# Graph network, first layer: attribute loads issued in one burst per group instead of in lots of four

## The chip, the cores and the metric

The kernel runs on one core of one Trainium2 chip. The metric is the device time in microseconds of one execution. The engines are TensorE (PE, with its weight loads shown as PEld), VectorE (DVE), ScalarE (ACT), GpSimd (POOL) and SyncE (SP). DMAs are issued from the queues of SP, ACT and POOL; "SPq" and "ACTq" in the profile are the instructions of these queues that issue them.

## The reference, cut to what matters

Four blocks run one after the other on 6250 nodes with 256 features, each adding its result to x: a message-passing layer over 106250 edges, a mixture of experts routed by a graph attention, a second message-passing layer, and a second mixture of experts. The change lies in the first of them:

```python
def _L0_gnn_ref(x, edge_index, edge_attr, u, batch, W1, b1, W2, b2):
    row, col = (edge_index[0], edge_index[1])
    h = jnp.concatenate([x[row], edge_attr], axis=1)
    h = jax.nn.relu(h @ W1 + b1)
    agg = jax.ops.segment_sum(h, col, num_segments=N_NODES)
    cnt = jax.ops.segment_sum(jnp.ones((h.shape[0],), h.dtype), col, num_segments=N_NODES)
    agg = agg / jnp.maximum(cnt, 1.0)[:, None]
    out = jnp.concatenate([x, agg], axis=1)
    return jax.nn.relu(out @ W2 + b2)

x = x + _L0_gnn_ref(_layernorm(x, axis=-1), edge_index, edge_attr_256, ...)
```

All arrays are float32; edge_attr has 106250 rows of 256. The edges are sorted by their target node (col).

## The kernel before

Before the layer, a short stage makes y = layernorm(x) @ W1[:256] + b1 for all nodes and writes it to DRAM (`y_dram`). Then the layer walks over windows of 128 target nodes. There are 49 windows; since the edges are sorted, each window's edges are one run of rows, and the kernel takes 18 tiles of 128 edges for each, cut into three groups of six tiles. So there are 147 groups (`groups1`), and the loop over q is what the change touches. The windows come in seven blocks of seven.

For a group q, the work on the engines is this:

- `load_sources(q)`: six gathers on POOL (`gather`, L1184) bring the rows of y of the edges' source nodes into one of four buffers (`ring`, tile h). The gathers for group q+2 stand in iteration q; the buffer was last read by `add_up(q - 2)`.
- `load_attr(q)`: the attribute rows (tile ea, three buffers) come by 12, 12 or 8 DMAs, for the three groups of a window in turn. Each covers 32 partitions in rows of 256 bytes. The order of their engines is SP, ACT, SP, ACT in each run of four, and SP alone in a third run; so a group has 8, 8 or 4 on SP and always 4 on ACT. The first row of the window is read from a table (`start_of`, L1094) into a register of both queues.
- `turn(q)` (L1613): DVE transposes the loaded rows in blocks of 32 (et <- ea). It stands one iteration ahead of its use, and frees the buffer of ea.
- `hidden(q, j)`: PE multiplies two tiles with the lower half of W1 (helper `mm`, L1170, ph <- w1b, et); three calls make the group.
- `join(q)`: DVE adds the product to the gathered rows (L1631, h <- ph, h), ACT applies relu (L1632).
- `equal(q)`: DVE compares the edges' targets with the lanes of the window (L1283); `add_up(q)`: PE adds the rows up per node (L1650), two iterations after the group's products.

Beside that, three generators advance by one step at fixed places of an iteration (`steps`):

- `work`: the end of a window (`end_of`): mean (ACT L1663, o), transposes (PE L1164, copied by ACT L1165), product with W2, layer norm for the next block (ACT L1685 ln_rs, DVE L1687 and L1689, ACT L1691 xn, named o in the profile), and the attention's scores (ACT L1702 to L1704). All its small products and transposes share one PSUM buffer.
- `sort`: the sort of the attention's edges by DVE, at the end with transposes and writes of the sorted rows through ACT (L1435 to L1438, low_dram).
- `slow`: `windows()`: counting, then once per block `find_starts` (L1091) and `load_windows`, whose first step reads seven windows' source and target indices on SP: seven reads of `start` (L1094) and fourteen DMAs (L1202, raw_src and raw_dst). These index reads fall into the iterations 8, 23, 37, 51, 65 and 79.

The order of the instructions on every engine is the program's order: `ordered.pin()` at the end of each iteration ties each instruction to the one before it on its engine, DMA issues included. Loads are prepared four groups ahead: iteration q prepares group q+4 once `turn(q + 1)` has freed a buffer, so that what `load_attr` issues waits for that transpose.

In the kernel before, `load_attr` issues nothing itself; it returns the list of its DMAs, and `issue(parts, 4)` takes four from the list at three places of an iteration: after the gathers and before `turn(q + 1)`, in the middle after `hidden(q, 2)`, and at the end after `steps(slow)`. The layer begins with a list of two groups; after eight iterations it is so short that a group's first four leave in the middle of the iteration that prepared it, the next four at its end, and the last four, all of SP, at the first place of the next iteration. ACT's two pairs thus stand on both sides of the work step in the middle of the iteration.

Of the kernel before, what the change touches and what calls it, by code (L numbers as in the profile page):

```python
# [918 lines left out]
def kernel(ctx: ExitStack, tc: tile.TileContext, a: dict, out: bass.AP):  # L919
# [73 lines left out]
    V, SC, TE, GP, SY = nc.vector, nc.scalar, nc.tensor, nc.gpsimd, nc.sync  # L993
# [7 lines left out]
    with ExitStack() as fast:  # L1001
# [23 lines left out]
        def bcast_row(pool, name, ap):  # L1025

            n = ap.shape[0]
            t = pool.tile([P, n], F32, name=name)
            SY.dma_start(t, bass.AP(tensor=ap.tensor, offset=ap.offset, ap=[[0, P], [1, n]]))
            return t  # L1030

        def load_rows(pool, name, ap):

            r, n = ap.shape
            t = pool.tile([P, r // P, n], F32, name=name)
            SY.dma_start(t, ap.rearrange("(c p) n -> p c n", p=P))
            return t
# [13 lines left out]
        if T1 > C1:  # L1051
            V.memset(flat.bitcast(I32)[:, C1:T1], 2**24)
            n = E1 - C1 * P
# [39 lines left out]
        def start_of(w, *also):  # L1093
            return nc.values_load(  # L1094
                start[0:1, w : w + 1], engines=(mybir.EngineType.SP, *also), min_val=0,
                max_val=E1 - WE, skip_runtime_bounds_check_because="it is clamped to that",
            )
# [17 lines left out]
        def load_nodes(engine, t0, t1):  # L1115
            for ps, tt, rows in node_parts(a["x"], t0, t1):
                engine.dma_start(x_all[ps, tt, :], rows)
# [18 lines left out]
        def norm_scale(pool, t0, n):  # L1136

            mv = pool.tile([P, n, 2], F32, name="ln_mv")
            for i in range(n):
                st = pool.tile([P, 6], F32, name="ln_st")  # L1140
                V.bn_stats(st, x_all[:, t0 + i, :])
                V.bn_aggr(mv[:, i, :], st)
            rs = pool.tile([P, n], F32, name="ln_rs")
            V.tensor_scalar(rs, mv[:, :, 1], EPS, None, op0=OP.add)
            SC.activation(rs, rs, AF.Sqrt)
            V.reciprocal(rs, rs)
            return mv, rs
# [12 lines left out]
        def transposed(psum, dst, src, n=2):  # L1160

            pt = psum.tile([P, n, P], F32, name="pt")
            for c in range(n):
                TE.transpose(pt[:, c, :], src[:, c * P : (c + 1) * P], ident)  # L1164
            SC.activation(dst, pt.rearrange("p c k -> p (c k)"), AF.Copy)  # L1165

        def mm(dst, lhs, rhs, n=2):

            for c in range(n):
                TE.matmul(dst, lhs(c), rhs(c), start=c == 0, stop=c == n - 1)  # L1170
# [154 lines left out]
        def load_keys():  # L1325

            for i, raw in enumerate((key, order)):
                edge = a["L0_ffn_edge_index"][i, :].rearrange("(p t) -> p t", t=C2)
                SY.dma_start(raw.bitcast(I32), edge)
# [118 lines left out]
        with ExitStack() as layer:  # L1448
# [45 lines left out]
            def load_attr(q):  # L1494

                w, g = groups1[q]
                parts = []
                ea = wea.tile([P, G1 * 4, 2 * Q], F32, name="ea")
                r = start_of(w, mybir.EngineType.Activation)
                rows = a["edge_attr_256"][bass.ds(r, WE), :]  # L1500
                at = 0
                for i, (first, n) in enumerate(RUNS[g]):
                    part = rows[first * P : (first + n) * P, :]
                    for c in (0, 2, 1, 3):
                        parts.append((
                            SY if c < 2 or i == 2 else SC,
                            ea[c * Q : (c + 1) * Q, at : at + 4 * n, :],
                            part[:, 2 * c * Q : 2 * (c + 1) * Q].rearrange(
                                "(m p) d -> p m d", p=Q
                            ),  # L1510
                        ))
                    at += 4 * n
                return ea, parts

            def issue(parts, n):

                for engine, to, part in parts[:n]:
                    engine.dma_start(to, part)
                del parts[:n]


            with (
                tc.tile_pool(name="w0", bufs=1) as w0,
                tc.tile_pool(name="n0", bufs=3) as wk,
                tc.tile_pool(name="pt0", bufs=3, space=PSUM) as pst,
                tc.tile_pool(name="p0", bufs=3, space=PSUM) as psm,
                tc.tile_pool(name="pq0", bufs=1, space=PSUM) as psq,
            ):
                w1a = load_rows(w0, "w1a", a["L0_gnn_W1"][0:D, :])
                b1 = bcast_row(w0, "b1", a["L0_gnn_b1"])  # L1530
                for b in range(1, NB):
                    load_nodes(SY, b * TB, (b + 1) * TB)
                ahead = {}
                for t0, t1 in parts0:
                    b = t0 // TB
                    mv, rs = norm_scale(wk, t0, t1 - t0)
                    off = wk.tile([P, TB], F32, name="off")
                    V.scalar_tensor_tensor(
                        off[:, 0 : t1 - t0], mv[:, :, 0], -1.0, rs, op0=OP.mult, op1=OP.mult
                    )  # L1540
                    for i in range(t1 - t0):
                        t = t0 + i
                        xn = wk.tile([P, D], F32, name="xn")
                        SC.activation(
                            xn, x_all[:, t, :], AF.Identity, bias=off[:, i : i + 1],
                            scale=rs[:, i : i + 1],
                        )
                        xt = b_all[:, t, :]
                        transposed(pst, xt, xn)
                        pm = psm.tile([P, D], F32, name="pm")  # L1550
                        mm(pm, lambda c: xt[:, c * P : (c + 1) * P], lambda c: w1a[:, c, :])
                        yb = wk.tile([P, D], F32, name="yb")
                        V.tensor_add(yb, pm, b1)
                        SY.dma_start(y_nodes[:, t, :], yb)
                    if t1 == TB:
                        for w in range(TB):
                            count_below(w)
                        find_starts(psq, 0)
                    if b == 1:
                        b2, w1b, w2, *of_gat = load_weights(w0)  # L1560
                        for _ in load_windows(0, psq):
                            pass
                    if b == 2:
                        load_keys()
                    if b == 4:
                        wgx = with_scores(w0, *of_gat)
                    if b >= 4:
                        ahead[b - 4], parts = load_attr(b - 4)
                        issue(parts, len(parts))


            HS = D + 4
            with (
# [24 lines left out]
                NQ1 = len(groups1)  # L1598
# [137 lines left out]
                for q in range(3):  # L1736
                    load_sources(q)
                turn(0)
                LOT = 4
                ordered = Ordered(tc)  # L1740
                for q in range(NQ1 + 2):
                    if 0 < q <= NQ1:
                        join(q - 1)
                    if q < NQ1:
                        hidden(q, 0)
                    steps(keys or sort)
                    if q >= 2:
                        add_up(q - 2)
                        if (q - 2) % NG == NG - 1:
                            work.append(end_of((q - 2) // NG))  # L1750
                    if 3 <= q + 2 < NQ1:
                        load_sources(q + 2)
                    issue(parts, LOT)
                    if q + 1 < NQ1:
                        turn(q + 1)
                    for n in range(q + 2, min(q + 5, NQ1)):
                        if n not in ahead:
                            ahead[n], more = load_attr(n)
                            parts += more
                    if q < NQ1:  # L1760
                        hidden(q, 2)
                    issue(parts, LOT)
                    steps(keys or (sort if q % 4 else []))
                    if q < NQ1:
                        equals[q] = equal(wk, *groups1[q])
                        hidden(q, 4)
                    steps(slow)
                    issue(parts, LOT)
                    ordered.pin()
                while work or sort or slow:  # L1770
                    steps(sort, slow)
# [110 lines left out]
        part = sums.tile([P, 3, T, H], BF16, name="part")  # L1882
        with (
# [17 lines left out]
            for at in range(0, NM * P, D):  # L1901
                n = min(D, NM * P - at)
# [882 lines left out]
        with (  # L2785
# [6 lines left out]
            n = wk.tile([P, NB + 7], F32, name="n")  # L2792
# [61 lines left out]
```

## Time and profile before

| | us |
|---|---|
| median of 10 runs | 3302.36 |
| lowest, highest | 3299.53, 3311.06 |
| the profiled execution, its own time | 3304.03 |
| its span, first to last instruction | 3302.2 |
| first gather of the layer, last relu's end | 102.0, 1260.2 |
| busy in the span: PE, DVE, POOL, ACT | 3004.0, 2185.4, 2277.2, 1184.6 |

The whole profile is of one execution. A line of a group or of a timeline gives the start and length of an instruction, its engine, its line in the kernel, what it writes and reads, and in brackets how long its engine stood idle before it and what ended that. The release is inferred from semaphores; "issue" means that the profile shows nothing that was waited for. DMA-issuing instructions are not counted as busy, and merged lines give the time from the first to the last of them.

### The profile page before, as it was taken

To read this page: it belongs to the slowest core of one execution; us is meant where nothing else is said; L and a number is where in the kernel's file an instruction comes from. 1 tells how busy PE (TensorE), PEld (TensorE's weight loads), DVE (VectorE), ACT (ScalarE), POOL (GpSimd) and SP (SyncE) were. 2 spreads that over 40 slices of the span, in tenths; PEclk is the share of its full clock that TensorE was granted. 3 is DMA by queue.
4 is the path that set the end of the run, shared out by engine and by line. 5 is a ranking of instruction groups with operands and counts; after the bars stand their busy time and mean duration, and the time that the engine had idled before them with its cause. 6 is when DMAs were issued, how large, how long until landed. Compare 5 with 4: busy or idle time off the path is not lost.

```text
span 3302.2 us, 59987 instructions
## 1 busy us (share of the span) xinstructions
PE 3004.0 (91%) x18517; PEld 2361.5 (72%) x18517; DVE 2185.4 (66%) x6516; ACT 1184.6 (36%) x2200; POOL 2277.2 (69%) x2720
## 2 busy tenths in 40 slices
PE   6899999999999989999999999956788888889997
PEld 5677777777777767888888888844566666656675
DVE  6678887888777766887685869962344444444464
ACT  5122222222222223456666668840112112112234
POOL 1577777777777774777776677427777777777772
PEclk8999999999999999999999999965577777777798
DMA  5788998989998873445454535532222222222221
GB/s 176 190 195 196 201 207 191 199 198 205 206 206 204 193 180 101 114 104 137 108 145 107 142 96 154 134 102 53 53 59 59 59 60 55 64 60 59 60 66 30
DMA packets 704935, 423.34 MB, mean 128 GB/s; under 512 B 538699, under 2 KB 647303, under 8 KB 704604
## 3 DMA queue, kind: packets, MB, share of 16 engines
q1 hardware_dynamic: 422972, 201.12, 23.3%
q0 software_dynamic: 88512, 171.58, 22.9%
q10 hardware_dynamic: 193120, 46.69, 7.0%
q8 instruction: 150, 2.46, 0.3%
q14 instruction: 181, 1.48, 0.2%
HBM read 382.75 MB, written 42.50 MB: 129 GB/s over the span
## 4 chain that ended last, share of the span: by engine, by line
PE 57%; POOL 14%; DMA 11%; issue 9%; DVE 5%; ACT 2%; SPq 2%; ACTq 0%; DVEq 0%; POOLq 0%
PE ph L1170 30%; POOL hg L1184 12%; PE py L1170 11%; PE pe L1650 4%; PE pt L1170 4%; DMA hg<-hp_dram,src 3%; PE pe L2714 3%; DMA ea<-in_edge_attr_dram 3%; DMA h<-y_dram,src 1%; PE po L2032 1%; POOL sg L1184 1%; DMA rb<-low_dram 1%; PE pt L1164 1%; PE pa L1955 1%; SPq L1202 1%
## 5 line engine op out<-in xcount | busy, mean ns | idle before, releaser
L1184 POOL DMA_INDIRECT h<-y_dram,src x882 | 860.6, 976 | 368.7 <-issue 212.1
L1184 POOL DMA_INDIRECT hg<-hp_dram,src x831 | 784.8, 944 | 280.5 <-issue 237.4
L1170 PE MATMUL ph<-w1b,et 128*128 128x256 f32 x3528 | 832.0, 388 | 14.7 <-DVE et L1613 9.5
L1184 POOL DMA_INDIRECT sg<-gat_dram,src x612 | 612.0, 1000 | 267.3 <-issue 166.5
L1170 PEld LDWEIGHTS ph<-w1b,et 128*128 128x128 f32 x3528 | 659.7, 192 | 162.3 <-issue 76.1
L2714 PEld LDWEIGHTS pe<-eq,hg 128*128 128x128 f32 x2036 | 397.4, 260 | 295.4 <-issue 142.8
L2714 PE MATMUL pe<-eq,hg 128*128 128x96 f32 (+15 forms) x2036 | 452.7, 354 | 147.9 <-DMA hg<-hp_dram,src 124.2
L2691 DVE TENSOR_SCALAR eq<-px,dst,ew 128x96 f32<-128x96 f32 x831 | 262.6, 369 | 247.1 <-PE pe L2714 145.6
L1170 PE MATMUL py<-w,hh 128*128 128x256 f32 x1568 | 399.5, 393 | 11.7 <-ACT hh L1833 10.3
L1170 PE MATMUL ph<-b_all,w 128*128 128x256 f32 (+1 forms) x1600 | 402.2, 388 | 1.0 <-ACT hh L1833 1.0
L1632 ACT ACTIVATE h<-h 128x1536 f32<-128x1536 f32 x147 | 218.4, 1486 | 503.5 <-DVE h L1631 249.5
L1631 DVE TENSOR_TENSOR h<-ph,h 128x1536 f32<-128x1536 f32 x147 | 258.2, 1756 | 170.4 <-PE ph L1170 123.3
L1170 PEld LDWEIGHTS py<-w,hh 128*128 128x128 f32 x1568 | 282.0, 192 | 49.6 <-ACT hh L1833 15.4
L1170 PEld LDWEIGHTS ph<-b_all,w 128*128 128x128 f32 x1600 | 284.1, 192 | 30.7 <-ACT hh L1833 1.5
L1613 DVE STREAM_TRANSPOSE et<-ea 128x1536 f32<-128x1536 f32 x147 | 260.8, 1774 | 14.6 <-DMA ea<-in_edge_attr_dram 9.7
L1833 ACT ACTIVATE hh<-ph,b 128x256 f32<-128x256 f32 (+1 forms) x400 | 166.9, 466 | 125.6 <-PE ph L1170 106.0
L2010 DVE TENSOR_SCALAR E<-nodes,bits 128x256 bf16<-128x256 bf16 (+5 forms) x612 | 187.8, 348 | 35.6 <-PE po L2032 34.2
L1650 PE MATMUL pe<-h,eq 128*32 128x257 f32 x2496 | 180.8, 394 | 0.0
L1833 ACT ACT_TABLE_LOAD x102 | 130.9, 1283 | 22.8 <-PE ph L1170 12.5
L1165 ACT ACTIVATE b_all<-pt 128x256 f32<-128x256 f32 x147 | 54.0, 377 | 214.9 <-PE pt L1164 211.4
L1170 PE MATMUL py<-ew,g 65*128 65x256 f32 x392 | 128.7, 457 | 1.0 <-DVE miss L2799 1.0
L1650 PEld LDWEIGHTS pe<-h,eq 128*32 128x32 f32 x2496 | 72.6, 111 | 69.5 <-issue 35.2
(358 smaller groups left out, 3941.8 us busy)
## 6 DMA issues: line engine op xcount, KB each, us to landing
ea<-in_edge_attr_dram SPq DMA_DIRECT2D x784, 64.0 KB
ea<-in_edge_attr_dram ACTq DMA_DIRECT2D x392, 64.0 KB
w<-in_L_ffn_W_dram SPq DMA_DIRECT2D x48, 512.0 KB
y<-ys SPq DMA_DIRECT2D x96, 256.0 KB
rb<-low_dram SPq DMA_DIRECT2D x84, 256.0 KB
ea<-in_edge_attr_dram ACTq DMA_DIRECT2D x196, 96.0 KB
ea<-in_edge_attr_dram SPq DMA_DIRECT2D x196, 96.0 KB
h<-y_dram,src POOLq DMA_INDIRECT x882
```

The source lines that it names most:

```text
L1164: TE.transpose(pt[:, c, :], src[:, c * P : (c + 1) * P], ident)
L1165: SC.activation(dst, pt.rearrange("p c k -> p (c k)"), AF.Copy)
L1170: TE.matmul(dst, lhs(c), rhs(c), start=c == 0, stop=c == n - 1)
L1184: GP.indirect_dma_start(out=dst, out_offset=None, in_=table[0:NP, :], in_offset=IndirectOffsetOnAxis(ap=idx, axis=0), **more,)
L1613: V.transpose(et[q].rearrange("p c m k -> p m c k"), ahead.pop(q).rearrange("p m (c k) -> p m c k", c=2),)
L1631: V.tensor_add(h, ph.pop(q), h)
L1632: SC.activation(h, h, AF.Relu)
L1650: TE.matmul(sums[w][b * Q : (b + 1) * Q, :], some[:, (b - lo) * Q : (b - lo + 1) * Q], rows_of(q)[:, j, 0:WS], start=(g, b, j) in begin, s ...
L1833: SC.activation(hidden[u][:, f, :n, :], ph[:, f - f0, :n, :], AF.Gelu, bias=b1[:, e, f : f + 1],)
L2010: V.tensor_scalar(Es[g, j][:, 0:n, :].rearrange("p b k -> p (b k)"), nodes16[:, 0 : n * P], bits.bitcast(F32)[:, g * G + j : g * G + j + 1 ...
L2691: V.tensor_scalar(equals[k][:, j, :], lanes[:, 0:NW], dst_of[:, t : t + 1], ew[:, t : t + 1], op0=OP.is_equal, op1=OP.mult,)
L2714: TE.matmul(sums[b][:, lo - t0 * P : hi - t0 * P], hg[:, j, :], eq[:, j, lo - n0 : hi - n0], start=False, stop=after >= (t0 + n) * P,)
```

## The change

`load_attr` issues its DMAs itself, in the same order and on the same engines, and is called at the end of an iteration, after the steps of `slow`. The list of pending DMAs, `issue` and its three places are gone. The stage before the layer, which loads the first three groups, issues the same DMAs as before.

```diff
             def load_attr(q):
 
                 w, g = groups1[q]
-                parts = []
                 ea = wea.tile([P, G1 * 4, 2 * Q], F32, name="ea")
                 r = start_of(w, mybir.EngineType.Activation)
                 rows = a["edge_attr_256"][bass.ds(r, WE), :]
...
                     for c in (0, 2, 1, 3):
-                        parts.append((
-                            SY if c < 2 or i == 2 else SC,
+                        (SY if c < 2 or i == 2 else SC).dma_start(
                             ea[c * Q : (c + 1) * Q, at : at + 4 * n, :],
                             part[:, 2 * c * Q : 2 * (c + 1) * Q].rearrange(
                                 "(m p) d -> p m d", p=Q
                             ),
-                        ))
+                        )
                     at += 4 * n
-                return ea, parts
-
-            def issue(parts, n):
-
-                for engine, to, part in parts[:n]:
-                    engine.dma_start(to, part)
-                del parts[:n]
+                return ea
...
                     if b >= 4:
-                        ahead[b - 4], parts = load_attr(b - 4)
-                        issue(parts, len(parts))
+                        ahead[b - 4] = load_attr(b - 4)
...
                 turn(0)
-                LOT = 4
                 ordered = Ordered(tc)
...
                     if 3 <= q + 2 < NQ1:
                         load_sources(q + 2)
-                    issue(parts, LOT)
                     if q + 1 < NQ1:
                         turn(q + 1)
-                    for n in range(q + 2, min(q + 5, NQ1)):
-                        if n not in ahead:
-                            ahead[n], more = load_attr(n)
-                            parts += more
                     if q < NQ1:
                         hidden(q, 2)
-                    issue(parts, LOT)
                     steps(keys or (sort if q % 4 else []))
                     if q < NQ1:
                         equals[q] = equal(wk, *groups1[q])
                         hidden(q, 4)
                     steps(slow)
-                    issue(parts, LOT)
+                    for n in range(q + 2, min(q + 5, NQ1)):
+                        if n not in ahead:
+                            ahead[n] = load_attr(n)
                     ordered.pin()
```

## The prediction

> **What bounds the kernel now.** I read the page's first part and its groups, then tables of busy time by stretch, then, inside the first layer (102 to 1257 us of the span), the timelines of POOL, ACT, SP and PE one at a time. On the page:
>
> ```profile
> PE 3004.0 (91%) x18517; PEld 2361.5 (72%) x18517; DVE 2185.4 (66%) x6516; ACT 1184.6 (36%) x2200; POOL 2277.2 (69%) x2720
> ...
> L1184 POOL DMA_INDIRECT h<-y_dram,src x882 | 860.6, 976 | 368.7 <-issue 212.1
> ```
>
> By shares PE is the bound. Busy time by stretch (columns: stretch, length, busy time of PE, PEld, DVE, ACT, POOL, then clock, DMA share, GB/s) gives this for the first layer:
>
> ```profile
> 250.00:500.00 250.00, 244.68 (x1536) 190.61 (x1534) 216.29 (x459) 72.22 (x121) 187.25 (x194) 0.99 0.92 202
> 500.00:750.00 250.00, 240.43 (x1469) 186.81 (x1470) 203.15 (x411) 67.71 (x113) 186.01 (x190) 0.97 0.89 195
> ```
>
> PE is busy 96 to 98% and POOL only 75%, but POOL's share deceives. Its timeline shows gathers of 0.94 to 1.0 us with 0.30 us between two that no wait explains (in brackets: idle time before):
>
> ```profile
> 307.19 0.95 POOL L1184 DMA_INDIRECT h<-y_dram,src  x1 [0.30 <-issue]
> 309.99 0.94 POOL L1184 DMA_INDIRECT h<-y_dram,src  x1 [1.86 <-issue]
> ...
> 319.10 0.95 POOL L1184 DMA_INDIRECT h<-y_dram,src  x1 [1.92 <-issue]
> ```
>
> 0.976 + 0.30 is 1.276 us a gather, 7.66 us a group of six, and 147 groups make 1126 us. From the first gather at 102.0 to the last one's end at 1245.9 are 1143.9 us. So POOL's string of gathers has hardly a hole: adding up what each gather idled over 0.30 us gives about 15 us. PE alone is a little faster: after a stall it gains back some 0.4 us a group (add joins lag behind landed gathers by 10.6 us at group 85 and by 0.3 us at 113). The layer therefore ends when POOL does, plus PE's lag at the end (8.6 us), and a stall of PE costs time only where it makes POOL wait for a buffer. That happened at groups 27 and 28, just shown (1.56 and 1.62 us too much). Why it happened is on ACT, SP and PE:
>
> ```profile
> 292.52 3.86 ACTq L1518 DMA_DIRECT2D ea<-in_edge_attr_dram  x4
> 297.43 1.48 ACT L1632 ACTIVATE h<-h 128x1536 f32<-128x1536 f32 x1 [5.45 <-DMA ea<-in_edge_attr_dram]
> 299.23 0.20 ACT L1685 ACTIVATE ln_rs<-ln_rs 128x1 f32<-128x1 f32 x1 [0.31 <-DVE ln_rs L1684]
> 305.84 1.63 ACTq L1518 DMA_DIRECT2D ea<-in_edge_attr_dram  x2
> 307.59 0.60 ACT L1691 ACTIVATE o<-x_all,off,ln_rs 128x256 f32<-128x256 f32 x1 [8.16 <-DMA ea<-in_edge_attr_dram]
> ```
>
> ```profile
> 286.03 7.33 SPq L1518 DMA_DIRECT2D ea<-in_edge_attr_dram  x6
> 294.41 0.33 SPq L1202 DMA_DIRECT2D raw_src<-in_src_dram  x1
> ...
> 304.55 0.28 SPq L1202 DMA_DIRECT2D raw_dst<-in_dst_dram  x1
> 305.04 7.82 SPq L1518 DMA_DIRECT2D ea<-in_edge_attr_dram  x12
> ```
>
> ```profile
> 299.99 5.45 PE L1170 MATMUL ph<-w1b,et 128*128 128x256 f32 x24
> 308.24 0.44 PE L1164 MATMUL pt<-ident,o 128*128 128x128 f32 x2 [2.80 <-ACT o L1691]
> 308.61 2.28 PE L1650 MATMUL pe<-h,eq 128*32 128x257 f32 x20
> 310.82 4.59 PE L1170 MATMUL ph<-w1b,et 128*128 128x256 f32 x16
> ```
>
> Once per block of seven windows (groups 8, 23, 37, 51, 65, 79) SP reads fourteen index rows (294.41 to 304.83 here, 1.5 us a pair). The DMAs of SP and ACT use eight completion semaphores in turn, and each issue waits in its engine's queue for the DMA eight before it. So the first lot of the next group's attribute loads on ACT (305.84) waits for the last index reads, and with it ACT's xn (L1691), which had its inputs at about 301; PE waits from 303.7 to 308.24 for that, and POOL later for PE.
>
> **The change part by part.** (1) Loads on SP. In the steady state group q+4's loads wait for the transpose that frees their buffer, wherever they stand; SP has nothing else to do then. Its 980 issues keep their times: 0.
>
> (2) The first lot of two on ACT moves behind the work steps of its group. In one group of three these steps end 3.1 us later (289.11 against 286.03), so these loads start 3 us later. Cover: that group is issued by 290 and its transpose starts at 306.5, some 12 us after landing; in the whole run the transposes waited this little for loads:
>
> ```profile
>   DMA ea<-in_edge_attr_dram: 9.7, 39
> ```
>
> (us, times.) Cost 0; without the cover 3 us for 49 groups, 147 us. The Trainium skill's "DMA: Bandwidth & Descriptors", section "Rules for kernel authors", speaks against the change: issue a DMA early and wait for it late. By that rule the move would lose part of those 147 us; the row says none.
>
> (3) Four issues instead of two stand just ahead of the next relu on ACT (0.55 us each). In the group of three with late steps the relu comes some 0.7 us late: last issue over at about T+5.4 against relu at T+4.7, T being the end of the freeing transpose. Hidden: its reader on PE comes a group later, and the copy queued behind it on ACT is read 3 us later. Cost 0; uncovered 0.7 x 49 = 34 us.
>
> (4) The index reads now stand ahead of all loads of group q+4 on SP and no longer wait for its buffer. In block 2 they can start at 288.4 (earlier loads issued at 287.9, starts computed at 288.3) instead of 294.4, and end at about 299.1. The four ACT loads, behind them in turn, are held until the reads land, 297 to 301; relu goes from 297.4 to 298 to 301, ln_rs to 300 to 302.5, xn to 301.5 to 304. PE is there at 303.7: a stall of 0 to 0.5 us for one of 4.5. The same holds where xn (blocks 1 and 5) or the window's mean and score copies (block 4: ACT L1663 idled 8.28 us) stood behind the first lot: PE gains 4 to 5 us in each.
>
> (5) It loses in blocks 3 and 6. There relu of the same group was on time before (407.1 and 735.8) and will be held until the reads land (414 and 741 to 742.5), with the copies behind it that PE needs: about 2.6 us net in block 3, 5.5 in block 6 (3.6 to 7).
>
> What PE gains counts where POOL had waited. Idle over 0.30 us after block 2: 1.6 + 1.6 + 0.3; after block 4: 0.5 + 2.7 + 1.2; after block 5: 0.7; after block 6: 1.3. The first three vanish: 3.5 + 4.4 + 0.7 = 8.6 us. Block 6 keeps its 1.3: PE's lag there, 10.8 us, grows by 5.5 but begins some 4 us smaller. POOL begins to idle at a lag near 12 us. Bounds: 9.9 us gained if block 6 is harmless too; nothing if ACT is held as long as now.
>
> (6) The end of the layer. At groups 138 to 141 the sorted keys' rows go out through ACT one after another, each waiting for the one before to land (3.3 to 3.9 us). The first of these no longer stands behind two loads (1.1 us earlier), and relu 138 stands behind four (up to 0.9 later): 0, bounds -1.1 and +0.9. (7) The start: loads come up to 9 us earlier, the string of gathers starts at 102.0 as now: 0, bounds within 1 us either way.
>
> Sum: 8.6 us less than the profiled execution's 3304.0 (span 3302.2), 3295.4. That execution lies 1.7 us over the median of the runs, 3302.4; from the median 3293.8 us. The clock adds little: after that stall 16 matmuls took 4.59 us against 3.72 in the steady state, at a granted clock of 0.97 to 0.99 in these stretches. The skill's "TensorE: Matmul & The Clock Gate", Part 1, says an idle PE falls to half clock and needs about 3.4 us of work to recover. By it every stall removed would give back up to 1.7 us more; it would go into PE's lag, not into POOL's string.
>
> **The rivals.** *No net change.* ACT's hold only moves from the next group's first lot to this group's end; PE's stall moves with it and POOL idles as long as now: 3300 to 3303. For it: ACT is held in every block in either order. Against it: the reads start 3 to 6 us earlier, and what PE waited for is no longer behind the loads.
>
> *Slower: the four loads on ACT hold relu and the copies behind it past POOL's slack.* This decides if the index reads do not start earlier, so that ACT stands until the last one lands (306.2 in block 2, 416.7 in block 3, 745.7 in block 6). Then PE loses 1.7 us in blocks 2 and 5, 2 in block 4, 7.5 in block 3 and 10 in block 6 over today. With lags of 11 to 13 us already there, all but some 4 us of block 3's goes to POOL: 1.7 + 1.7 + 2 + 3.5 + 10 = 19 us, 3321; half of it, 3312, if the holds fall in between. It decides from about 4 us of lag added in a block.
>
> *The change does nothing*: loads are issued by buffer and semaphore, not by place, and the blocks' stalls are not on POOL's path. Same number as no change; counted there.
>
> **How the numbers follow.** About 0.2%, 6.6 us, is what a measurement of this kernel can tell from no change. Forecast, mostly over that line: faster 0.47. No net change, with forecasts that give only 2 to 6 us: 0.27. Slower: 0.26; the first layer has so many waits in turn that a hold I have not seen is likelier than a gain I have not seen. Range: from 3288 (9.9 gained, 1.1 at the end, and 3.6 us of POOL's idle time at groups 141 to 143) to 3314, which leaves out the worst half of the slower case.
>
> **What would show it.** Right: POOL's idle over 0.30 us between 290 and 760 falls from 10 us to under 2; index reads start at about 288 and 505.7; ACT's xn and L1663 no longer idle on loads, and relu at the blocks' own groups does; PE stalls at group 80 grow to 7 us. Wrong: POOL idle as long as before, or relu's wait for loads (140 us in 32 waits now) more than doubled with PE waiting for its copies, or transposes waiting for loads.

## The result and the profile after

The changed kernel takes 3316.4 us in the median of 10 runs (3311.0 to 3320.6), the kernel before 3303.2 in runs beside them: ratio 1.0039, 95% interval 1.003 to 1.0047. It is slower by some 13 us. The profiled execution (span 3310.2 us, its own time 3312.0) lies near the lowest of its runs, so its trace shows 8 of these 13.

All of it is in the first layer. From the end of the last gather to the end of the span both traces have 2056.3 us. The string of gathers took 1154.4 us (99.5 to 1253.9) instead of 1143.9, with the same work in it; on the page:

```profile
L1184 POOL DMA_INDIRECT h<-y_dram,src x882 | 859.5, 974 | 376.7 <-issue 211.9
```

The idle time over 0.30 us, summed over the gathers of the layer, grew from 15.4 us to 26.8, and it moved. POOL's timeline of the changed kernel after blocks 2, 3 and 6 (in brackets the idle time before the gather):

```profile
304.27 1.51 POOL L1184 DMA_INDIRECT h<-y_dram,src  x1 [0.79 <-issue]
...
313.38 0.94 POOL L1184 DMA_INDIRECT h<-y_dram,src  x1 [1.05 <-issue]
...
418.77 0.95 POOL L1184 DMA_INDIRECT h<-y_dram,src  x1 [5.35 <-ACT ln_rs L1676]
...
750.11 0.95 POOL L1184 DMA_INDIRECT h<-y_dram,src  x1 [8.59 <-issue]
...
761.00 0.96 POOL L1184 DMA_INDIRECT h<-y_dram,src  x1 [3.57 <-ACT ln_rs L1676]
```

The two gaps after block 2 shrank from 1.9 to 0.8 and 1.1; those at groups 41 and 82 are new, and the one at 83 has grown (it was 1.3 us over 0.30). The chain behind the largest stands in block 6. Before, on ACT and on PE:

```profile
735.84 1.48 ACT L1632 ACTIVATE h<-h 128x1536 f32<-128x1536 f32 x1 [2.05 <-DMA h<-y_dram,src]
737.23 0.58 ACT L1395 ACTIVATE order<-pt 128x512 f32<-128x512 f32 x1
...
741.38 7.00 ACTq L1518 DMA_DIRECT2D ea<-in_edge_attr_dram  x4
```

```profile
737.86 0.44 PE L1164 MATMUL pt<-ident,o 128*128 128x128 f32 x2 [2.17 <-ACT order L1395]
```

After, on SP, ACT and PE (relu is L1623 here):

```profile
731.78 1.86 SPq L1504 DMA_DIRECT2D ea<-in_edge_attr_dram  x4
734.22 0.33 SPq L1202 DMA_DIRECT2D raw_src<-in_src_dram  x1
...
743.88 0.28 SPq L1202 DMA_DIRECT2D raw_dst<-in_dst_dram  x1
```

```profile
741.13 4.25 ACTq L1504 DMA_DIRECT2D ea<-in_edge_attr_dram  x4
745.66 1.48 ACT L1623 ACTIVATE h<-h 128x1536 f32<-128x1536 f32 x1 [10.47 <-DMA ea<-in_edge_attr_dram]
747.05 0.58 ACT L1395 ACTIVATE order<-pt 128x512 f32<-128x512 f32 x1
```

```profile
747.68 0.69 PE L1164 MATMUL pt<-ident,o 128*128 128x128 f32 x2 [10.60 <-ACT order L1395]
748.30 1.94 PE L1641 MATMUL pe<-h,eq 128*32 128x257 f32 x16
```

The four loads of the burst stand on ACT behind the fourteen index reads in the turn of the eight semaphores, and relu and the copy `order` behind the four loads. Before, both were done when ACT came to its held loads. PE waits 10.6 us for the copy instead of 2.2. Behind it stand the sums of group 78 (748.30), which free the buffer for POOL's gathers of group 82 (750.11).

Two more readings say how it happened. PE's time for the four groups from each block's own one on (37.0, 34.5, 30.8, 37.4, 33.7 and 34.4 us before, from the end of one group's products to the end of the next's) changed by -4.5, +0.9, +6.0, -0.8, +0.7 and +9.7 us. And the index reads started little earlier, measured from the end of the transpose that frees the buffer: 4.5, 1.9, 1.4, 1.5, 1.4 and 1.4 us after it in the kernel before, and 0.6, 1.9, 0.2, -1.0, 0.8 and 1.6 in the changed one; in blocks 2 and 6 no earlier at all. From the first read to relu it took 11.4 to 12.6 us in all six blocks of the changed kernel, so with these reads and loads in a row it is the start of the reads that decides when relu leaves. Block 2 in the changed kernel, SP and ACT:

```profile
281.88 0.32 SPq L1504 DMA_DIRECT2D ea<-in_edge_attr_dram  x1
287.80 0.33 SPq L1202 DMA_DIRECT2D raw_src<-in_src_dram  x1
```

```profile
282.82 1.89 ACTq L1504 DMA_DIRECT2D ea<-in_edge_attr_dram  x4
...
299.79 1.48 ACT L1623 ACTIVATE h<-h 128x1536 f32<-128x1536 f32 x1 [13.05 <-DMA ea<-in_edge_attr_dram]
```

SP has issued its last load at 282.2 and stands until 287.7. By its semaphore the first read waits for the first of the four loads of the group before on ACT, which the change put behind that iteration's copies (issued at 282.82) and which landed at 287.67. The freeing transpose ended at 285.9. In block 6 it was SP's own last four loads that stood for such a load, from 728.0 to 731.8, with the reads behind them.

### The profile page after: what moved, and what is told of

The parts are those of the page before. It is cut to its first block, busy times and chain, and to the rows that moved or that the text cites. A ratio compares the mean times of both kernels' runs of the same rounds, so it can differ in the third digit from the quotient of the medians.

```text
span 3310.2 us, 59965 instructions
## 1 busy us (share of the span) xinstructions
PE 2999.7 (91%) x18517; PEld 2361.1 (71%) x18517; DVE 2182.6 (66%) x6516; ACT 1183.4 (36%) x2200; POOL 2274.2 (69%) x2720
## 4 chain that ended last, share of the span: by engine, by line
PE 55%; POOL 14%; DMA 11%; issue 9%; DVE 6%; ACT 2%; SPq 2%; ACTq 0%; DVEq 0%; POOLq 0%
PE ph L1170 30%; POOL hg L1184 13%; PE py L1170 10%; DMA ea<-in_edge_attr_dram 5%; PE pe L1641 4%; PE pt L1170 3%; PE pe L2700 3%; DMA hg<-hp_dram,src 3%; PE po L2018 1%; POOL sg L1184 1%; PE pa L1941 1%; PE pt L1164 1%; DMA rb<-low_dram 1%; DVE et L1604 1%; DVE E L1996 1%
## 5 line engine op out<-in xcount | busy, mean ns | idle before, releaser
L1623 ACT ACTIVATE h<-h 128x1536 f32<-128x1536 f32 x147 | 218.3, 1485 | 573.9 <-DMA ea<-in_edge_attr_dram 242.0
L1170 PE MATMUL py<-w,hh 128*128 128x256 f32 x1568 | 399.0, 393 | 11.9 <-ACT hh L1819 10.5
```

The source lines that it names most:

```text
L1623: SC.activation(h, h, AF.Relu)
```

## The experiments

Theory A: the loss is ACT standing behind the block of index reads. Rival B: the burst costs a little in every group. Columns: median, ratio to the kernel before in the same runs with its 95% interval, length of the string of gathers in the profiled execution, and POOL's idle time over 0.30 us at blocks 1 and 2, at 3, at 4 and 5, at 6, and at the end (groups 137 to 146). Medians are of runs on several chips, on which the kernel before took 3301.1 to 3303.5 us, so that small differences between them are good to some 2 us. String and idle time are of one execution each; those of the changed kernel and of e17_late_lots lie 4.5 and 6.6 us under their medians, that of e18_single_sp 5.7 under, those of e10_single_before and e12_all_sp 3.2 and 4.6 over.

| run | median | ratio | string | 1+2 | 3 | 4+5 | 6 | end |
|---|---|---|---|---|---|---|---|---|
| before | 3303.2 | 1 | 1143.9 | 4.8 | 0.0 | 5.3 | 1.3 | 4.0 |
| after | 3316.4 | 1.0039 (1.003 to 1.0047) | 1154.4 | 1.7 | 5.3 | 6.3 | 11.8 | 1.7 |
| e1_two | 3309.0 | 1.0024 (1.0013 to 1.0034) | 1147.0 | 4.3 | 2.0 | 6.3 | 4.4 | 2.9 |
| e2_six | 3320.4 | 1.0051 (1.0037 to 1.0065) | 1161.3 | 10.6 | 0.7 | 13.6 | 5.9 | 1.9 |
| e3_phase | 3308.8 | 1.0023 (1.0014 to 1.0032) | 1147.8 | 5.6 | 1.5 | 4.7 | 7.8 | 1.5 |
| e4_middle | 3321.6 | 1.0063 (1.0049 to 1.0076) | 1164.9 | 9.3 | 2.7 | 13.4 | 4.6 | 7.3 |
| e9_single | 3287.9 | 0.9953 (0.9939 to 0.9968) | 1131.7 | 0.0 | 0.0 | 0.0 | 0.3 | 2.8 |
| e10_single_before | 3294.4 | 0.9973 (0.9964 to 0.9982) | 1137.3 | 0.0 | 0.0 | 0.0 | 0.0 | 6.0 |
| e11_split | 3293.0 | 0.9967 (0.9954 to 0.9979) | 1132.4 | 0.0 | 0.0 | 0.0 | 0.7 | 1.6 |
| e12_all_sp | 3295.6 | 0.9978 (0.9969 to 0.9987) | 1135.8 | 0.0 | 0.0 | 6.9 | 0.0 | 2.6 |
| e13_reads_36 | 3299.2 | 0.9992 (0.9983 to 1.0001) | 1141.9 | 3.5 | 0.0 | 6.1 | 3.7 | 1.8 |
| e14_reads_1245 | 3295.5 | 0.9977 (0.9968 to 0.9986) | 1137.4 | 0.0 | 1.5 | 0.4 | 4.5 | 2.8 |
| e15_prev_sp | 3307.0 | 1.0009 (0.9997 to 1.002) | 1147.8 | 0.0 | 1.9 | 4.9 | 10.0 | 1.6 |
| e16_reads_last | 3322.3 | 1.0057 (1.0044 to 1.0071) | 1162.8 | 8.6 | 3.7 | 17.8 | 1.2 | 3.9 |
| e17_late_lots | 3294.1 | 0.9979 (0.997 to 0.9987) | 1132.2 | 0.0 | 0.0 | 0.0 | 2.3 | 0.5 |
| e18_single_sp | 3307.7 | 1.0017 (1.0008 to 1.0026) | 1142.7 | 0.0 | 0.0 | 11.8 | 3.7 | 0.8 |

**Taking ACT's loads away where the reads are.** The changed kernel, with

```diff
-            def load_attr(q):
+            def load_attr(q, alone=False):
-                        (SY if c < 2 or i == 2 else SC).dma_start(
+                        (SY if c < 2 or i == 2 or alone else SC).dma_start(
...
-                            ahead[n] = load_attr(n)
+                            ahead[n] = load_attr(n, q in (37, 79))
```

> The changed kernel, but in iterations 37 and 79 (blocks 3 and 6) the burst's four loads on ACT are issued by SP. Theory A (the loss is ACT held at these four loads behind the index reads, with relu and the copies behind it, in these two blocks: POOL idled 5.3 us at group 41 and 8.6 + 3.6 us at groups 82 and 83 in the changed kernel, 0 and 1.3 in the kernel before): about 15 us come back, 3316.4 - 15 = 3301, and POOL idles under 2 us over 0.30 at groups 41, 82 and 83. Rival B (the burst costs in the steady state: relu late in every third group, loads later in all): two of 147 iterations change nothing, 3313 to 3318. Rival C (the blocks' stall sits in SP's index reads as such, whoever is behind them): between 3310 and 3318, with the idle time at the same groups.

Half of it came back, 7.4 us. relu 37 and 79 (those of groups 37 and 79) were on time, but the next ones, 38 and 80, started 7.8 and 7.9 us after their join: the next group's loads on ACT left between 416.0 and 420.3 in block 3, behind SP, which by then had the reads and eight loads to issue. The hold had moved on by one group. With all six iterations (`q in (8, 23, 37, 51, 65, 79)`):

> As the run before, in all six iterations with index reads (8, 23, 37, 51, 65, 79). Theory A: blocks 1, 2, 4 and 5 still hold relu 5 to 11 us in the changed kernel, but POOL idles only some 8 us there in all; of that 4 to 6 come back too: 3295 to 3298, below the kernel before (3303). Rival B: 3313 to 3318. Rival C: no better than 3310.

The run missed: 3320.4. relu 24 waited 11.1 us after its join and relu 52 10.1, worse than in the changed kernel. In blocks 1, 2, 4 and 5 moving the loads only lengthens SP's lag, and ACT waits for it a group later. Both theories were too simple in one point: ACT is not held by its own loads' place alone, but by SP's lag.

**Other places.** One empty step before the reads of blocks 3 to 6 (`if b >= 3: yield` ahead of `load_windows`):

> The changed kernel with one empty step more before the index reads of blocks 3, 4, 5 and 6, so that all reads fall into iterations 8, 23, 38, 53, 68 and 83, where the window's end does its layer norm step (the place at which blocks 1 and 2 lost little). ACT is held as long as in the changed kernel. Theory A in the form that the place decides, since in blocks 3 and 6 the copy that PE's single buffer waits for stands behind relu: POOL idles under 2 us per block, 3316.4 - 13 = 3303 or a little less. If the length of the hold alone decides, wherever it falls: 3312 to 3318. Rival B: 3313 to 3318.

7.6 us back, 13 expected. Block 3 idled 1.5 us instead of 5.3, block 6 still 7.8. And block 2, in which nothing differs from the changed kernel, idled 5.6 us here, 3.8 in e1_two, 3.5 in e13_reads_36 and 1.7 in the changed kernel's own profile: that profile is likely a lucky one, which would be why it shows only 8 of the 13 us. The burst ahead of the work step in the middle, and just ahead of the reads (the `for n` loop moved up):

> One burst as in the changed kernel, but right after the transpose of the group, where the list was made up in the kernel before: it stands ahead of the work step in the middle and of the index reads. Theory A: the index reads hold the next group's ACT loads, and with them the layer norm's copy and relu, as in the kernel before: 3301 to 3308. Rival B (a burst of four on ACT ahead of relu costs, wherever it stands): 3311 or more.

> The changed kernel with the burst just ahead of the step that reads the indices instead of behind it: the reads then hold the next group's loads on ACT. If the place of the held ACT loads against relu and the copies decides: relu of the blocks' own groups is on time as in the kernel before, the next group's is held some 8 us, PE loses about what it lost in the kernel before, 3300 to 3308. If any hold of this length costs alike: 3314 to 3320.

Theory A missed in both, at 3322. e4_middle lies in rival B's range and e16_reads_last 2 us above that of its rival, yet POOL did not idle between groups 100 and 136 in either, so this is no cost in every group. In e16_reads_last relu of the blocks' own groups was on time in five blocks of six (0.7 us late in block 6), as expected, but blocks 1, 2, 4 and 5 idled more than before. The place ahead of relu is not the whole cause: a burst loses on either side of the reads.

**Splitting the reads.** Two windows, or one, in each step of `load_windows`, in the changed kernel and in the one before:

```diff
                     SY.dma_start(v[at : at + CW, :], rows)
-            for _ in range(3):
+                if b:
+                    yield
+            for _ in range(0 if b else 3):
                 yield
```

(one window; for two, `if b and (w - b * TB) % 2: yield`, and the three empty steps stay.)

> The changed kernel with the fourteen index reads of a block (b > 0) split over four iterations, two windows (four reads) in each. Theory A (all of the loss is ACT standing behind a block of fourteen reads, 10.3 us long; outside the blocks the burst costs nothing): the hold falls to some 3 us in each of four groups, within the slack, and POOL's 25 us of idle time over 0.30 at the blocks nearly vanish: 3316.4 - 22 = 3294. Rival B (the burst costs in the steady state): 3308 or more. Rival D (SP has no room: 4 reads of 0.75 us beside 8 loads make every load of these groups late, and the stall is only spread): 3305 to 3316.

> The same split in the kernel before. Theory A: its 11 us of POOL's idle time at the blocks vanish too, 3302 - 10 = 3292, the same as e5_split within 4 us, since then nothing is left in which the lots and the burst differ. Rival B: 3292, and e5_split stays 10 us or more above it.

> The changed kernel with one window's two reads in each of seven iterations (and without the two empty steps that followed the reads). Theory A: no hold over 1.5 us, POOL idle at the blocks under 2 us in all: 3290 to 3294. Rival B: 3308 or more. Rival D: as e5_split or worse.

> The same in the kernel before. Theory A: 3289 to 3294, equal to e7_single within 4 us. Rival B: 10 us or more below e7_single.

These four runs tell nothing on the theories. On their chip the kernel before took 4198.6 us, and they took 4186.2, 4189.8, 4193.8 and 4181.5 (ratios 0.9984, 1.0003, 1.0006 and 0.9975, each interval reaching 1). In their profiles a gather still takes 0.97 us and a join 1.76, but DVE's joins idled 305 us instead of 180 in e11_split, and POOL idled in nearly every group (some 1.8 us a group over 0.30, so that a group took 9.5 us instead of 7.7). The granted clock was lower, 0.84 against 0.89, but PE's products took 395 ns instead of 386, far too little for that. Why waits were longer there stays open. Three of the kernels ran again:

> The same kernel as e7_single, again: the four runs before it fell on a chip on which the kernel before takes 4199 us and the first layer is short of loads in every group, so that they say nothing on holds of a few us. Theory A: 3290 to 3294, POOL idle at the blocks under 2 us in all. Rival B: 3308 or more. Rival D (no room on SP): 3300 to 3316 with small idle times in many groups.

> The same kernel as e8_single_before, again. Theory A: 3289 to 3294, within 4 us of e9_single. Rival B: 10 us or more below e9_single.

> The same kernel as e5_split, again. Theory A: 3294; four reads in an iteration hold ACT some 3 us. Rival B: 3308 or more. Rival D: 3305 to 3316.

Theory A's reading holds in all three, rival B falls: without a block of reads the burst costs nothing, and POOL idles 0.0 to 0.7 us at all blocks together. e9_single lies 2 us below its range, e10_single_before 0.4 above. In e9_single the first window's reads pass between the loads, and ACT has its four loads out in 3 us:

```profile
170.04 0.34 SPq L1202 DMA_DIRECT2D raw_src<-in_src_dram  x1
170.61 0.29 SPq L1202 DMA_DIRECT2D raw_dst<-in_dst_dram  x1
171.81 4.37 SPq L1506 DMA_DIRECT2D ea<-in_edge_attr_dram  x8
```

```profile
170.47 2.97 ACTq L1506 DMA_DIRECT2D ea<-in_edge_attr_dram  x4
174.56 1.49 ACT L1625 ACTIVATE h<-h 128x1536 f32<-128x1536 f32 x1 [4.61 <-DMA ea<-in_edge_attr_dram]
```

The expected tie missed: e9_single is 6.5 us below e10_single_before. Their two profiles lie 9.4 us apart in span. Of this 3.2 us are POOL's idle time at the end of the layer (2.8 against 6.0), at groups 141 and 142, where ACT writes the sorted rows (no run took these writes apart); 3.6 us lie behind the last gather, where the loads have no part.

**All loads on SP** (`load_attr(n, True)`), with the reads in one block, and with single reads:

> The changed kernel with every attribute load on SP, none on ACT; the fourteen reads stand in one block. Theory A as first put (the hold of ACT is the loss, whatever SP does): 3290 to 3297, POOL idle under 4 us at the blocks. Theory A as the runs with two and six iterations have changed it (SP falls 10 us behind at the reads, and whoever shares its turn or needs its loads waits): SP has 12 issues of 0.65 us a group, 7.8 us against 7.66, in two groups of three and 5.2 in the third, so it makes up only some 0.7 us a group, transposes wait for loads after every block: 3305 to 3330.

> e9_single with all attribute loads on SP. Nothing is left that holds ACT, and POOL already idles only 0.3 us at the blocks in e9_single: if that is so, no more to gain in the blocks, 3285 to 3291, the same as e9_single within 3 us. If SP has no room for 12 loads and two reads in a group: 3292 to 3300, with transposes that wait for loads.

The first hits the time of theory A as first put, though POOL idled 6.9 us at the blocks and not under 4: with no load of its own ACT is no longer held at the reads (relu of the blocks' own groups and of the next two followed its join at once), and the kernel gains 6.8 us on the one before. SP issued a load every 0.51 us where nothing was waited for, not every 0.65, so twelve take 6.1 us. But the transposes now wait for loads, 63.3 us in 53 waits, and POOL idles 5.4 us at block 5. The second missed both ways: 20 us above e9_single. There the single reads queue on SP behind the loads; DVE waited 14.0 us in three waits for a block's last reads, the transposes 53.6 us for loads, and POOL idled 5.7 and 6.1 us at groups 56 and 74. The Trainium skill's "DMA: Bandwidth & Descriptors", section "Issuing engines are not separate DMA queues", says that issuing from several engines saves only the time to initiate a DMA, usually small beside the DMA. In e18_single_sp it is not small: by an estimate from these runs twelve loads of 0.51 us and a pair of reads of 1.5 us fill 7.6 of the 7.66 us of a group. In e12_all_sp it is not what was gained; there ACT no longer waited for semaphores.

**Which blocks, and what sets the reads' start.** In the next two the reads of some blocks alone are split over six steps (`if b in (3, 6) and w > b * TB: yield`, or `(1, 2, 4, 5)`); e15_prev_sp is e1's edit with `q in (7, 22, 36, 50, 64, 78)`.

> The changed kernel with the index reads of blocks 3 and 6 alone split over six iterations (the first step reads two windows, the next five one each). If the loss is in blocks 3 and 6: their 5.3 + 11.8 us of POOL's idle time go, 3316.4 - 16 = 3300, at or a little under the kernel before. If every block loses alike: a third comes back, 3308.

> The changed kernel with the index reads of blocks 1, 2, 4 and 5 split, those of 3 and 6 in one step as they are. If the loss is in blocks 3 and 6: the 8 to 12 us idle in the others go (also in the kernel before 10 us were idle there), 3304 to 3308, and 17 us of idle time stay at the two blocks left. If every block loses alike: 3299.

> The changed kernel, but in the iterations just ahead of the reads (7, 22, 36, 50, 64, 78) the burst is all on SP. If the reads start no earlier because the first of them waits for an ACT load of the group before, issued late behind ACT's copies: they start 1 to 4 us earlier against the freeing transpose, ACT is held that much less, 3306 to 3312. If something else sets their start: same phase (0 to 2 us behind the transpose) and 3314 to 3318.

e13_reads_36 hit, 17 us back, though block 6 still idled 3.7 us. e14_reads_1245 missed low: 21 us back, with blocks 3 and 6 as they were, only in iterations 43 and 91. Block 3's hold was not shorter there: relu 43 and 44 waited 10.5 and 8.6 us, and PE took 40.0 us for the four groups (36.8 in the changed kernel). But POOL idled only 1.5 us, as the blocks before had cost PE nothing: at group 43 the joins followed the landed gathers by 1.1 us, at group 37 of the changed kernel by 5.7. Holds share one slack, and their costs don't add. Block 6 also has the copy `order` behind relu only while the sort's transposes run, which iteration 91 no longer meets.

e15_prev_sp hit in time, 9.4 us back, and in two blocks by the reason given. In block 2, SP and ACT:

```profile
279.81 3.93 SPq L1504 DMA_DIRECT2D ea<-in_edge_attr_dram  x8
284.35 0.33 SPq L1202 DMA_DIRECT2D raw_src<-in_src_dram  x1
```

```profile
292.12 4.39 ACTq L1504 DMA_DIRECT2D ea<-in_edge_attr_dram  x4
296.79 1.48 ACT L1623 ACTIVATE h<-h 128x1536 f32<-128x1536 f32 x1 [11.21 <-DMA ea<-in_edge_attr_dram]
```

The reads start 1.8 us ahead of the transpose's end (286.2) instead of 1.9 behind it, 3.7 us earlier, and relu with them (10.6 us behind the transpose instead of 13.9). PE's four groups take 30.5 us there, against 35.0 to 38.7 in the changed kernel, e1_two, e3_phase and e13_reads_36, which have the same code at that block. In block 5 the reads start 2.5 us earlier, in block 1 0.6, in 3, 4 and 6 no more than 0.9 either way. In these last three the group before has twelve loads, and SP, with all of them, issued about as long as it had before issued and waited, so the run cannot tell there. At block 6 POOL's idle time stayed (10.0 us); at block 3 it fell from 5.3 to 1.9 us with a hold as long as before.

**The row of four.** The kernel before with its lots one place later: the list is made at the end of an iteration, behind the index reads, and issued in fours there and at the next two places:

```diff
-                    for n in range(q + 2, min(q + 5, NQ1)):
-                        if n not in ahead:
-                            ahead[n], more = load_attr(n)
-                            parts += more
...
                     steps(slow)
+                    issue(parts, len(parts))
+                    for n in range(q + 2, min(q + 5, NQ1)):
+                        if n not in ahead:
+                            ahead[n], more = load_attr(n)
+                            parts += more
                     issue(parts, LOT)
```

> The kernel before with its lots one place later: a group's first four loads at the end of the iteration, behind the step of the index reads, as in the changed kernel; the next four at the first place of the next iteration, behind relu and the copies; the rest in the middle of it. If the row of four on ACT is what costs: relu waits for two held loads only, some 3 us less in every block (in block 6 of the changed kernel ACT's loads left at 741.1, 742.2, 743.7 and 745.0): 3305 to 3311. If the place ahead of relu costs, with two loads as with four: 3313 to 3318.

3294.1, 22 us below the changed kernel and 11 better than the more hopeful expectation. The first loads stand where the change put them; ACT's pairs are apart, and SP's lots with them. The index reads start where they did in the changed kernel (2.4, 2.1, 0.1, -0.4, 1.4 and 1.2 us after the transpose), and relu leaves 1.8 to 4.3 us earlier against it in all six blocks. In block 6, on ACT, PE and POOL (line numbers of the kernel before):

```profile
723.52 1.72 ACTq L1518 DMA_DIRECT2D ea<-in_edge_attr_dram  x2
725.52 1.48 ACT L1632 ACTIVATE h<-h 128x1536 f32<-128x1536 f32 x1 [6.63 <-DMA ea<-in_edge_attr_dram]
726.91 0.58 ACT L1395 ACTIVATE order<-pt 128x512 f32<-128x512 f32 x1
728.33 0.39 ACT L1165 ACTIVATE o<-pt 128x256 f32<-128x256 f32 x1 [0.84 <-PE pt L1164]
728.65 4.37 ACTq L1518 DMA_DIRECT2D ea<-in_edge_attr_dram  x4
```

```profile
727.54 0.69 PE L1164 MATMUL pt<-ident,o 128*128 128x128 f32 x2 [6.75 <-ACT order L1395]
```

```profile
740.27 0.96 POOL L1184 DMA_INDIRECT h<-y_dram,src  x1 [2.41 <-ACT ln_rs L1685]
```

ACT waits for two loads, does relu and the copies, and waits for the other two with nothing urgent behind them. relu leaves 9.3 us after the freeing transpose (716.2), against 13.1 in the changed kernel; PE's wait falls from 10.6 to 6.75 us and POOL's from 8.59 + 3.57 to 2.41, the only idle time left at any block in this execution. Only 3.9 us of this is PE's shorter wait. PE also entered block 6 with less lag, since the blocks before had cost less: the joins followed the landed gathers by 0.7 us at group 79, against 6.6 in the changed kernel.

## Why the prediction was wrong

I forecast 3293.8 us; it was 3316.4, above my range, and the rival "slower" was right, nearly by its own condition: the index reads started much less early than I counted on, and in blocks 2 and 6 no earlier. Step by step:

- *What bounds the layer*: right. The medians follow the length of POOL's string within a few us, and its length follows the idle time at the blocks and at the end.
- *(1) to (3), loads and relu in the steady state cost nothing*: right. POOL did not idle at all between groups 100 and 136 in any run but those on the chip of e5 to e8, and with split reads the burst loses nothing.
- *(4), the failed step*: I let the reads start as soon as SP was through with its earlier loads (288.4 in block 2, 4.1 us ahead of the transpose's end) and forgot that they, and SP's loads ahead of them, also wait for the DMAs eight before them. Step (2) puts those, the previous group's loads on ACT, later. So in block 2 the reads started 1.9 us after the transpose's end, as before. The time of day came out nearly right, 287.8, only because that execution was 6.6 us ahead there; against the group it was 6 us off. ACT's hold ended with relu 13.9 us after the freeing transpose in block 2, where I had 5.5 to 8.5. The length of the hold was not the fault: 11.4 to 12.6 us from the first read to relu, counted from the start that I forecast, would have given 7.3 to 8.5. Blocks 1, 2, 4 and 5, of which I expected 4 to 5 us of PE's time each, gave 4.5, -0.9, 0.8 and -0.7; and block 1's 4.5 is of one execution, since e1_two, e3_phase and e13_reads_36, with the same code there, took 36.0 to 37.2 us where the kernel before took 37.0. e15_prev_sp shows the cause in blocks 2 and 5: with those loads off ACT the reads start 3.7 and 2.5 us earlier, and the blocks give 4.0 and 2.5 us (PE 30.5 and 31.2 us against 34.5 and 33.7). In block 6 the wait of SP's last loads points to the same; in 1, 3 and 4 it is only argued.
- *The stall of block 2 in the kernel before* was misread: its line has PE idle for 2.80 us, from 305.44, not 4.5 from 303.7, where only 16 of the 24 products shown were over. About as much as forecast was to be had all the same: with single reads (e9_single) the four groups take 29.2 us instead of 34.5.
- *(5), mis-sized by the same error*: 2.6 and 5.5 us in blocks 3 and 6, measured 6.0 and 9.7. Block 6's reads started 1.6 us after the transpose as before (1.4), and relu left 13.1 us after it, where I had 9.9 to 11.4. The rival's prices, 7.5 and 10, were nearer. Nor did PE enter block 6 with 4 us less of lag: 6.6 us at group 79, 6.9 before.
- *The rule by which stalls reach POOL* (a lag near 12 us) held: with joins 14.1 us behind the landed gathers at group 39 and 19.9 at group 80 POOL lost 5.3 us, and 11.8 where it had lost 1.3. What I missed is how much of the hold is the row's own, four loads behind the reads instead of two: e17_late_lots keeps the place of the first loads and the start of the reads, without the row, and takes 3294.1. That this is what I forecast for the change is chance. Neither the row nor the block costs this alone: with the row and split reads (e9_single, e11_split) POOL hardly idles at the blocks either.
- *(6), the end*: put at 0 within -1.1 and +0.9; POOL idled 2.3 us less there (1.7 against 4.0), and 3.2 less with single reads, so it was mis-sized a little. *(7), the start*: 99.5 against 102.0, but the string started between 97.8 and 103.3 in these runs, with no link to the edit that I can see.
- *What would show it*: of the signs for "wrong", POOL idled 25.1 us at the blocks instead of 11.4. relu's wait for loads (between 150 and 1250 us) grew from 140 to 207 us, less than the doubling I had named, but PE's waits for ACT's copies did grow; the transposes' waits for loads did not (10.1 us against 9.7):

```profile
PE pt L1164 <- ACT order L1395: 10.6, 1, 10.6
...
PE pt L1170 <- ACT o L1165: 5.8, 2, 4.8
```

The best version found is e9_single, the change with one window's reads in each of seven iterations: 3287.9 us, 0.9953 of the kernel before. What stays open is block 6, where holds, sort and window end meet in an order that no run took apart: PE waits there for the copy `order` in every kernel, 1.2 us at the least (e12_all_sp) and 3.7 even with single reads (e9_single, e10_single_before). Nor did a run take apart why e4_middle and e16_reads_last are slower still.

## What to carry to other kernels

A DMA on a compute engine's queue is an instruction in that engine's order: before gathering such DMAs into one row, find the longest wait that the last of them can have (here for DMAs of another queue in the same turn of semaphores), and what is queued behind. When a moved DMA seems to start earlier, compute its start from the landing of the one whose semaphore it reuses, and measure it against the step that paces the loop, not against the clock of the trace. A block of small DMAs that delays two queues was better spread over the steps here than placed well, as long as its queue had room: with all loads on SP spreading lost (e18_single_sp 3307.7 us against e12_all_sp 3295.6). And where several holds share one slack, a saving at one shows at the next, so judge them by runs that take away one at a time and all together.

## What the runs showed of the hardware

- Two in-order queues that share a turn of completion semaphores delay each other both ways: in block 2 of the changed kernel SP stood 5.5 us for a load of ACT's (282.2 to 287.7), and ACT then 7.4 us for SP's reads ahead of its first load (286.7 to 294.2), and 13.05 us in all ahead of relu. The Trainium skill's "DMA: Bandwidth & Descriptors", section "Why a DMA increments its semaphore by 16 and not by 1", asks for one semaphore per DMA in flight. The trace agrees as far as that each semaphore is reused only after its DMA has landed (the load of 282.82 landed at 287.67, and the read that waited for its semaphore left at 287.80); what such a turn costs across two engines the section doesn't say.
- Fourteen reads of 9 KB take SP 9.9 to 10.9 us, 1.5 us a pair, although each `dma_start` takes only 0.3: between pairs SP loads the next start into a register (0.5 us) and its address.
- One chip took 4199 us for the kernel that takes 3302 on others, with the same time for each gather and join, a granted clock of 0.84 against 0.89, and longer waits between engines; there all four edits changed nothing that could be measured.
